# Four graph layers on one core: bias additions by accumulating DMA, an earlier place for the load of x, one more strip buffer and a new order of the steps

## Chip, cores and metric

The kernel runs on 1 core of one Trainium2 chip. The metric is the device time of one execution in microseconds, the median of three runs. A span is the time from the first to the last instruction of one profiled execution.

## The reference, cut to what matters

There are B = 32 graphs of N = 512 nodes with D = 256 features. Each passes through four layers in turn, and each layer ends in a residual and a layer norm. All is float32.

```python
x = layernorm(x + L0(x, adj))   # h = (1+eps)*x + adj @ x;  relu(h @ W1 + b1) @ W2 + b2
x = layernorm(x + L1(x, adj))   # graph attention, 4 heads, mask adj > 0.5, softmax, ... + bias
x = layernorm(x + L2(x, adj))   # attention, 8 heads of 32, scores + log(adj + 1e-6), ... @ Wo.T + bo
x = layernorm(x + L3(x, adj))   # softmax over (x W x^T) * adj with a node mask, times x
```

Three of the layers add a bias row of D numbers to every node's row: b2, bias and bo. These three additions are what the first part of the change is about.

## The kernel before

**Tiles.** A graph's x is one SBUF tile of 128 partitions by 4 chunks by 256 features, 4 KB in a partition. It is updated in place through all four layers, from its load (L667) to its store (L1436). The adjacency comes as four strips of 128 x 512, once for layer one (L660) and again for layer four (L1317). Layer one transposes the strips on TensorE (L685) into AT. Its first matmul that reads x is hT (L718), followed by h1T (L741) and y (L760).

**Tiling of TensorE.** Most matmuls use the whole 128 x 128 array. The scores of layer two's attention (s, L1105) are tiled by rows, four of 32 at once. Its sums (o_ps, L1163), and the denominators at L983, L1210 and L1232, are tiled by 32 columns, and layer one's attention (o_ps, L946) by 64 columns.

**Buffers.** There are four pools of interchangeable SBUF buffers: B (8 KB in a partition, 11 of them), C (4 KB, 12 of them: x, hT, xT, v, q, k and others take turns), D (2 KB, 17 of them: adjacency strips, nm, xs_row, exponentials of layer four) and the eight PSUM banks. A step that starts a tile takes a buffer and waits until an earlier owner is done with it.

**Order.** About six graphs are in work at once. Every piece of work is a named step with an engine, a duration, and the steps it comes after. `Plan.order` runs through them with these durations and picks, for the engine that is free, the step with the earliest due time. Due times are shifted by a table of moves that is written out in the last call, `plan.run`. The result is one fixed instruction order on each engine. So any change of a duration, of a buffer count or of the table changes the order everywhere. SyncE's DMA queue is in order too: a load that waits for its buffer holds up every load behind it.

**Bias.** `bias_bc` holds the three rows copied to all 128 partitions (3 KB in a partition). `bias_steps(k, after)` adds row k to x with four GpSimd operations, one for each chunk. Step `xb1` comes after hT, which needs x without the bias; `xb2` and `xb3` come after the transposes of x in layers two and three. The residual additions (L642, L1027) come after them.

**Denominators of layer two.** Eight tiles of exponentials are added up by accumulating DMAs that GpSimd issues (L1138, L1191), from SBUF to SBUF.

**Loads of a graph.** Steps `la0i` to `la3i` issue the four strips, and `lxi` issues x after `la3i`. `transfer` adds two steps that only count time: the queue and the landing.

Of the kernel before, what the change touches and what calls it, by code (L numbers as in the profile page):

```python
# [10 lines left out]
F32 = mybir.dt.float32  # L11
# [3 lines left out]
ALU = mybir.AluOpType  # L15
AX = mybir.AxisListType

P = 128
# [12 lines left out]
def row_bcast(ap, n):  # L31

    return bass.AP(tensor=ap.tensor, offset=ap.offset, ap=[[0, P], [1, n]])
# [194 lines left out]
def fast_path(  # L228
# [23 lines left out]
    nc = tc.nc  # L252
    B, N, D = x.shape
    NC = N // P
# [8 lines left out]
    const = ctx.enter_context(tc.tile_pool(name="const", bufs=1))  # L263
    sb = ctx.enter_context(tc.tile_pool(name="sb", bufs=1))
    small = ctx.enter_context(tc.tile_pool(name="small", bufs=1))
    dram = ctx.enter_context(tc.tile_pool(name="dram", bufs=3, space=bass.MemoryType.DRAM))
# [27 lines left out]

    wT = {n: const.tile([P, DC, D], F32, name=f"w{n}T") for n in ("q", "k", "v", "o")}
    w3_sb = const.tile([P, DC, D], F32, name="w3_sb")
    bias_bc = const.tile([P, 3, D], F32, name="bias_bc")


    def blk(i):  # L300
# [1 line left out]


    plan = Plan({
        "B": 11, "C": 12, "D": 17, "p": 8,

        "live": 6, "L0": 1, "L1": 2, "L2": 2, "L3": 1, "AT": 4, "zs": 7, "edge": 1, "tmp": 2,
    })
    step = plan.step
# [8 lines left out]
    def transfer(name, us, after, queue="q1", land=4.0):  # L318

        @step(f"{name}.q", queue, us, after)
        def _():
            pass

        @step(name, None, land, (f"{name}.q",))
        def _():
            pass


    def prepare():
        plan.graph()
        slot = plan.slot[0]
        t = {}
# [7 lines left out]
        def load(name, us, *transfers, take=(), little=False):  # L342


            @step(f"ld_{name}", "act" if little else "sp", 0.5 * len(transfers), take=take)
            def _():
                for transfer in transfers:
                    (nc.scalar if little else nc.sync).dma_start(*transfer())

            transfer(name, us, (f"ld_{name}",), "q3" if little else "q1", 2.0)  # L350
# [37 lines left out]
        load("w1", 2.5, lambda: (w1_sb, rows(w1)))  # L388
        load("w2", 2.5, lambda: (w2_sb, rows(w2)))

        def bias_row(k, b):
            return lambda: (bias_bc[:, k, :], row_bcast(b, D))

        load("bias", 0.6, *(bias_row(k, b) for k, b in enumerate((b2, gbias, bo))), little=True)

        def vector(name, a):
            def transfer():
# [159 lines left out]
    def graph(g):  # L557
# [3 lines left out]
        t = {"g": g}  # L561
# [16 lines left out]
        def bias_steps(k, after):  # L578


            @step(f"xb{k}", "pool", 2.7, after + ("^bias",))
            def _():

                for c in range(NC):
                    nc.gpsimd.tensor_tensor(  # L585
                        t["x"][:, c, :], t["x"][:, c, :], bias_bc[:, k - 1, :], ALU.add
                    )

        def norm_stats(n, c):
            nc.vector.bn_stats(t[f"st{n}"][:, c, :], t["xo" if n == 4 else "x"][:, c, :])  # L590
# [70 lines left out]

            transfer(f"la{c}", 1.0 if g == 0 else 2.0, (f"la{c}i",), land=4.0 if g else 2.0)

        @step("lxi", "sp", 0.45, (f"la{NC-1}i",), take=("C=x/2",))
        def _():
            t["x"] = mid("x", [P, NC, D], "x")
            nc.sync.dma_start(t["x"], x[g].rearrange("(c p) d -> p c d", p=P))  # L667
# [298 lines left out]
        for h in range(H1):  # L966
            after = (f"o1{h//2}0", f"zm{h}1")
            for k, m in enumerate((2, 1)):
# [6 lines left out]
                after = (f"as{h}0",)  # L975
# [470 lines left out]
    for g in range(B):  # L1446
        graph(g)
    with tc.manual_schedule():
        plan.run([(24, 0.1, 6, 100.0, ((959604, 5.0), (114893, 5.0), (536715, 2.0), (293975, 2.0), (179355, 2.0), (633130, 2.0), (136849, 2.0), (39540, 2.0)), (0.7, 0.3, 0.3), (('R', 7.0), ('Re', -17.0), ('Rl.q', 5.0), ('Rs.q', -24.0), ('Rsi', -4.5), ('Rt', -0.5), ('ab', 3.0), ('as00', -7.0), ('as01', 14.0), ('as10', 5.5), ('as11', 19.5), ('as20', -59.5), ('as21', 4.5), ('as30', -1.0), ('as31', -8.0), ('at0', 3.0), ('at1', 1.0), ('at2', 5.0), ('at3', 7.5), ('atd0', 5.0), ('atd1', -8.0), ('atd2', 0.5), ('atd3', 2.0), ('ate0', 6.0), ('ate1', 4.0), ('ate3', -93.0), ('cd1', 23.5), ('cd2', 24.0), ('cd3', 17.0), ('cd6', 34.5), ('cd7', 44.5), ('cq1', 31.5), ('cq2', 13.5), ('cq3', 2.0), ('cq5', 24.0), ('cq6', -16.0), ('cq7', -12.5), ('d1', -18.0), ('d2', -2.0), ('de', -81.5), ('dev1.0', -32.0), ('dev2.0', -18.0), ('dev3.0', -10.0), ('dev4.0', -53.0), ('e00', -9.0), ('e01', 0.5), ('e02', -5.0), ('e03', -9.5), ('e10', -17.5), ('e11', -4.5), ('e12', 3.5), ('e13', -20.0), ('e20', -111.5), ('e21', -50.0), ('e22', -3.5), ('e23', 7.5), ('e30', -17.0), ('e31', -1.0), ('e32', -16.0), ('e33', -46.0), ('e40', -115.0), ('e41', -5.0), ('e42', 7.0), ('e43', -11.0), ('e50', -8.5), ('e51', -8.5), ('e52', 3.0), ('e53', -3.0), ('e60', -13.5), ('e61', -27.0), ('e62', -6.0), ('e63', 1.0), ('e70', 7.0), ('e71', 54.5), ('e72', -2.0), ('e73', -20.0), ('ed0', 8.0), ('ed1', 11.5), ('ed2', -27.5), ('ed3', -0.5), ('f0', 10.0), ('f1', -2.0), ('f2', 3.5), ('f3', 7.0), ('fd0', 25.0), ('fd1', 6.5), ('fe0', -21.5), ('fe1', -44.5), ('fe2', -21.0), ('fe3', -12.0), ('fq0', -4.5), ('fq1', -2.0), ('h0', 0.5), ('h1', -34.5), ('he1', 4.5), ('hsb.q', -22.0), ('hsbi', 34.5), ('hsl', 10.0), ('i0', 8.5), ('i1', 6.0), ('ie0', -28.5), ('ie1', -15.5), ('k0', -31.0), ('k1', -56.5), ('ke0', 81.5), ('ke1', 87.0), ('la0.q', -176.5), ('la0i', -14.5), ('la1.q', -36.5), ('la2.q', -22.0), ('la3.q', -21.0), ('la3i', -9.0), ('lb0.q', 6.0), ('lb0i', -13.0), ('lb1.q', 4.5), ('lb1i', 38.0), ('lb2.q', 6.0), ('lb2i', -18.0), ('lb3.q', -6.0), ('lb3i', -3.5), ('ldni', -2.0), ('lx.q', 5.5), ('lxi', 8.0), ('m00', -14.0), ('m01', -4.0), ('m10', -24.0), ('m11', 2.0), ('m20', -51.5), ('m21', -8.0), ('m30', -29.0), ('m31', -19.0), ('m40', 9.0), ('m41', 4.0), ('m50', 30.0), ('m51', -2.5), ('m60', 12.5), ('m61', 28.0), ('m70', -1.0), ('m71', 2.5), ('n0', -1.5), ('n1', 2.0), ('n2', 1.5), ('n3', 4.5), ('n5', 0.5), ('n6', -28.5), ('n7', 8.5), ('nd0', 4.0), ('nd1', 36.5), ('no0', 9.0), ('no1', 8.5), ('node', 7.0), ('o100', 3.0), ('o101', -6.0), ('o110', 6.0), ('o111', 4.5), ('oe0', -1.0), ('oe1', 33.0), ('out0.q', 1.0), ('out0i', -5.5), ('p0', -2.0), ('p1', 7.5), ('q1', 1.0), ('qe0', -10.0), ('qe1', -12.0), ('r10', 119.5), ('r11', 3.5), ('r12', -10.0), ('r13', -19.0), ('r20', 161.0), ('r21', -13.0), ('r22', -3.5), ('r23', 25.0), ('r30', 83.0), ('r32', -1.0), ('r33', -6.0), ('r40', -2.0), ('r41', -12.0), ('r42', -9.0), ('rc00', 8.5), ('rc01', 3.0), ('rc10', 7.5), ('rc11', -27.0), ('rd1', -54.5), ('rd30', -59.0), ('rd31', 1.5), ('rd32', 2.5), ('s0', -1.0), ('s1', -16.0), ('s2', -0.5), ('s3', -21.5), ('s4', -35.5), ('s6', -24.5), ('s7', -2.0), ('sh1.0', -3.0), ('sh2.0', -12.5), ('sh3.0', 10.0), ('sh4.0', 7.0), ('st10', 16.5), ('st11', -1.0), ('st13', -29.5), ('st20', 15.0), ('st21', 35.5), ('st22', -0.5), ('st23', 27.5), ('st30', 50.0), ('st31', -14.0), ('st32', -9.0), ('st33', 15.5), ('st40', -4.5), ('st41', -9.5), ('st42', -2.0), ('st43', -3.0), ('t0', 0.5), ('t1', -2.5), ('t3', -12.0), ('ta0', -41.0), ('ta1', -0.5), ('ta2', -23.5), ('ta3', 3.0), ('tb0', -5.5), ('tb1', 1.0), ('tb2', 10.0), ('tb3', 23.5), ('te0', -13.0), ('te2', -5.0), ('te3', 26.0), ('u0', -1.0), ('u1', 7.0), ('u2', -2.0), ('u3', -55.0), ('ue0', -39.5), ('ue1', 16.5), ('ue2', -1.5), ('ue3', -17.0), ('v10', -3.5), ('v11', -16.5), ('v12', 5.5), ('v13', -5.0), ('v20', -50.0), ('v21', 10.5), ('v22', -10.0), ('v23', -5.0), ('va1.0', 15.5), ('va2.0', 7.5), ('va3.0', 0.5), ('va4.0', -24.5), ('ve10', -76.5), ('ve11', -11.5), ('ve12', -16.0), ('ve13', 0.5), ('ve20', -1.0), ('ve22', -23.0), ('ve23', -21.5), ('w0', 0.5), ('w1', 0.5), ('w3', 8.5), ('wx0', 32.5), ('wx1', -33.5), ('wx2', 18.5), ('wx3', 7.0), ('x10', -10.0), ('x11', 4.0), ('x30', -8.0), ('x31', -22.0), ('xb1', 1.0), ('xb2', -1.0), ('xb3', -3.5), ('xe10', -84.5), ('xe11', -134.0), ('xe20', -7.0), ('xe21', -5.5), ('xe30', -52.0), ('xe31', 12.0), ('xs.q', 10.5), ('xsi', 3.0), ('xt10', -6.5), ('xt11', -50.0), ('xt20', -73.5), ('xt21', -11.0), ('xt30', -4.0), ('xt31', 0.5), ('y0', 8.0), ('y1', -32.0), ('yd00', -41.5), ('yd01', 18.0), ('yd10', 11.0), ('yd11', 13.5), ('yn0', -82.0), ('yn1', -24.0), ('yn2', -25.0), ('yn3', -68.0), ('yt2', -0.5), ('z01', -48.5), ('z03', -6.0), ('z11', -0.5), ('z12', 2.0), ('z20', 1.0), ('z21', 2.5), ('z22', 3.0), ('z30', -57.5), ('z31', -38.0), ('z32', 5.0), ('z33', -3.0), ('zm00', -10.0), ('zm01', 29.0), ('zm11', 33.5), ('zm20', 24.0), ('zm21', 15.5), ('zm30', 10.0), ('zm31', 17.5)))])

# [470 lines left out]
```

## Time and profile before

| what | value |
|---|---|
| median of three runs | 2952.09 us (2947.92 to 2953.53) |
| the profiled execution's own time | 2948.64 us |
| its span | 2946.9 us |
| TensorE busy | 2890.2 us, 98% |
| VectorE busy | 2344.2 us, 80% |
| ScalarE busy | 1906.5 us, 65% |
| GpSimd busy | 704.4 us, 24% |
| granted TensorE clock | 0.998 |
| share of the DMA engines in the queue that GpSimd issues to | 40.7% |

In the profile, PE is TensorE's matmuls, PEld its weight loads, DVE VectorE, ACT ScalarE, POOL GpSimd, and SPq the DMA queue that SyncE issues to. `hT_ps<-AT,x L718` means that the instruction of line 718 writes hT_ps and reads AT and x. A list of waits names for each group of instructions what ended its engine's idle time, with the total, the number of waits and the longest. Where several things were waited for, the one that came last in the records is named. The chain of waits goes back from the last instruction, at each step to what released it. A wait on an engine that is not the bound costs nothing by itself.

### The profile page before, as it was taken

To read this page: it belongs to the slowest core of one execution; us is meant where nothing else is said; L and a number is where in the kernel's file an instruction comes from. 1 tells how busy PE (TensorE), PEld (TensorE's weight loads), DVE (VectorE), ACT (ScalarE), POOL (GpSimd) and SP (SyncE) were. 2 spreads that over 40 slices of the span, in tenths; PEclk is the share of its full clock that TensorE was granted. 3 is DMA by queue.
4 is the path that set the end of the run, shared out by engine and by line. 5 is a ranking of instruction groups with operands and counts; after the bars stand their busy time and mean duration, and the time that the engine had idled before them with its cause. 6 is when DMAs were issued, how large, how long until landed. Compare 5 with 4: busy or idle time off the path is not lost.

```text
span 2946.9 us, 42883 instructions
## 1 busy us (share of the span) xinstructions
PE 2890.2 (98%) x15521; PEld 1651.0 (56%) x15521; DVE 2344.2 (80%) x4389; ACT 1906.5 (65%) x3818; POOL 704.4 (24%) x782
## 2 busy tenths in 40 slices
PE   8999999999999999999999999999999999999998
PEld 6544665555655556555556555565555555555554
DVE  2878878877788877788777887778887778888796
ACT  3766766666666666666666666666576666666665
POOL 2322222122221222222222212222222222122210
PEclk9999999999999999999999999999999999999999
DMA  4166676455675456764557654567545576446651
GB/s 147 58 129 135 144 163 147 105 123 127 151 163 109 116 127 138 163 135 109 123 124 163 158 104 119 128 144 163 127 110 124 129 163 139 109 110 147 143 113 41
DMA packets 121467, 380.77 MB, mean 129 GB/s; under 512 B 12129, under 2 KB 52257, under 8 KB 89377
## 3 DMA queue, kind: packets, MB, share of 16 engines
q0 software_dynamic: 31744, 227.56, 40.7%
q1 hardware_dynamic: 88112, 149.75, 15.3%
q8 instruction: 125, 2.05, 0.3%
q10 hardware_dynamic: 1392, 0.66, 0.1%
q14 instruction: 94, 0.76, 0.1%
HBM read 133.30 MB, written 17.07 MB: 51 GB/s over the span
## 4 chain that ended last, share of the span: by engine, by line
PE 76%; DVE 14%; DMA 7%; ACT 2%; issue 1%; POOL 0%; POOLq 0%; SPq 0%; ACTq 0%; DVEq 0%
PE s L1347 8%; PE hT_ps L718 7%; PE o_ps L946 7%; PE h1T_ps L741 7%; PE y_ps L760 7%; PE s L1105 6%; DMA x<-in_x_dram 5%; PE o_ps L1163 5%; DVE z L1127 4%; PE iT_ps L1333 4%; PE v_ps L1086 3%; PE qT_ps L1068 3%; PE kT_ps L1068 3%; PE o2p_ps L1289 2%; PE xT_t L1049 2%; PE AT_t L685 2%
## 5 line engine op out<-in xcount | busy, mean ns | idle before, releaser
L1118 ACT ACTIVATE z<-s 128x512 f32<-128x512 f32 x1024 | 560.1, 605 | 164.2 <-PE o_ps L1163 107.2
L1127 DVE SCALAR_TENSOR_TENSOR z<-AT,z 128x1024 f32<-128x1024 f32 x512 | 618.1, 1216 | 48.3 <-ACT z L1118 48.2
L912 ACT ACTIVATE z<-R_bc,nT,S 128x512 f32<-128x512 f32 x512 | 390.3, 817 | 164.7 <-PE y_ps L760 138.1
L1138 POOL DMA_DIRECT2D z<-z x186 | 166.6, 898 | 1147.2 <-PE s L1105 329.1
L923 DVE SCALAR_TENSOR_TENSOR z<-z,T,edge 128x512 f32<-128x512 f32 x512 | 401.6, 829 | 45.4 <-ACT z L912 45.2
L585 POOL TENSOR_TENSOR x<-x,bias_bc 128x256 f32<-128x256 f32 x384 | 343.9, 994 | 211.4 <-PE xT_t L788 156.3
L631 ACT ACTIVATE x<-x,shift,rstd 128x256 f32<-128x256 f32 x508 | 285.1, 607 | 136.5 <-DVE shift L621 136.0
L613 POOL TENSOR_TENSOR rstd<-ve,nhalf 128x4 f32<-128x4 f32 (+1 forms) x131 | 147.7, 1128 | 806.7 <-DVE ve L607 792.9
L1105 PE MATMUL s<-qT,kT 32*128 32x512 f32 x2048 | 293.2, 639 | 4.1 <-ACT qT L1074 4.1
L1163 PE MATMUL o_ps<-z,v 128*32 128x512 f32 x2048 | 257.8, 600 | 0.2 <-DVE z L1127 0.2
L946 PE MATMUL o_ps<-z,v 128*64 128x512 f32 x1024 | 244.4, 605 | 0.2 <-DVE z L923 0.2
L1401 PE MATMUL o_ps<-x,eT 128*128 128x256 f32 x1024 | 233.5, 380 | 0.1
L1347 PE MATMUL s<-xT,iT 128*128 128x512 f32 x512 | 233.5, 599 | 0.0
L973 DVE TENSOR_TENSOR z<-z 128x1024 f32<-128x1024 f32 (+1 forms) x256 | 230.7, 953 | 2.0 <-PE o_ps L946 1.9
L741 PE MATMUL h1T_ps<-hT,w_sb 128*128 128x512 f32 x512 | 231.4, 593 | 0.0
L760 PE MATMUL y_ps<-w_sb,h1T 128*128 128x256 f32 x1024 | 226.9, 379 | 1.3 <-ACT h1T L747 1.3
L1253 DVE RECIPROCAL rdT<-rdT 128x256 f32<-128x256 f32 x128 | 221.5, 1738 | 7.1 <-ACT rdT L1246 7.1
L590 DVE BATCH_NORM_STATS2 st<-x 128x6 f32<-128x256 f32 x508 | 211.2, 416 | 9.3
L760 PEld LDWEIGHTS y_ps<-w_sb,h1T 128*128 128x128 f32 x1024 | 194.1, 190 | 39.3 <-issue 12.2
L718 PE MATMUL hT_ps<-AT,x 128*128 128x384 f32 (+2 forms) x768 | 209.8, 382 | 0.1
L1401 PEld LDWEIGHTS o_ps<-x,eT 128*128 128x128 f32 x1024 | 189.5, 190 | 30.2 <-issue 2.0
L1377 ACT ACTIVATE z<-z,nmax 128x512 f32<-128x512 f32 x128 | 92.4, 722 | 132.4 <-DVE nmax L1369 131.4
(155 smaller groups left out, 4234.8 us busy)
## 6 DMA issues: line engine op xcount, KB each, us to landing
z<-z POOLq DMA_DIRECT2D x186, 1024.0 KB, 8.1
A<-in_adj_dram SPq DMA_DIRECT2D x256, 256.0 KB
R_bc<-R_dram SPq DMA_DIRECT2D x32, 1024.0 KB
z<-z POOLq DMA_DIRECT2D x62, 512.0 KB, 6.0
x<-in_x_dram SPq DMA_DIRECT2D x32, 512.0 KB
out_dram<-x SPq DMA_DIRECT2D x31, 512.0 KB
nm<-in_nodemask_dram SPq DMA_DIRECT2D x32, 256.0 KB
xs_row<-xs_dram SPq DMA_DIRECT2D x32, 128.0 KB
```

The lines of the kernel that those rows point to most:

```text
L718: nc.tensor.matmul(ph[:, cols], t["x"][:, m, blk(d)], moving, start=(k == 0), stop=(k == len(parts) - 1),)
L741: nc.tensor.matmul(ph, w1_sb[:, d, blk(f)], t["hT"][:, d, :], start=(d == 0), stop=(d == DC - 1))
L760: nc.tensor.matmul(py[:, j, :], t["h1T"][:, f, blk(2 * c2 + j)], w2_sb[:, f, :], start=(f == 0), stop=(f == HC - 1),)
L912: nc.scalar.activation(t[f"e{h}"][:, c, :], t["Rbc"][:, h, :], AF.Relu, bias=t["nT"][:, h, c : c + 1], scale=t["S"][:, h, c : c + 1],)
L923: nc.vector.scalar_tensor_tensor(z, z, t["T"][:, h, c : c + 1], t["edge"][:, c, :], op0=ALU.add, op1=ALU.mult)
L946: nc.tensor.matmul(po[j * F1 : (j + 1) * F1, :], t["v"][:, c, h * F1 : (h + 1) * F1], t[f"e{h}"][:, c, :], start=(c == 0), stop=(c == NC - 1),
L1105: nc.tensor.matmul(pk, t["k"][hs, o, blk(c)], t["q"][hs, o, :], start=True, stop=True)
L1118: nc.scalar.activation(t[f"E{k}"][:, j, :], t[f"ps{k}{j}"], AF.Exp, scale=QSCALE)
L1127: nc.vector.scalar_tensor_tensor(z, t["AT"][:, c, None, :].to_broadcast([P, 2, N]), ADJ_EPS, z, op0=ALU.add, op1=ALU.mult,)
L1163: nc.tensor.matmul(t[f"n{o}"][32 * j : 32 * j + 32, :], t["v2"][:, c, o * P + F2 * j : o * P + F2 * (j + 1)], t[f"E{k}"][:, j, :], start=( ...
L1347: nc.tensor.matmul(pt, t["iT"][:, d, blk(c)], t["xT3"][:, d, :], start=(d == 0), stop=(d == DC - 1),)
L1401: nc.tensor.matmul(py, t[f"eT{c}"][:, blk(m)], t["x"][:, m, :], start=(m == 0), stop=(m == NC - 1),)
```

## The change

1. The bias tile in SBUF is gone. A DRAM tile `biases` holds each row four times in a line, written once by three small DMAs. For each graph and bias, GpSimd issues one DMA that reads that 4 KB line for each of the 128 partitions and adds it to x in place. The step `xb{k}` is split into `xd{k}` (the issue), `xq{k}` (the queue) and `xb{k}` (the landing).
2. `lxi` comes after `la0i`, the first strip, where it came after the last.
3. The D pool has 18 buffers where it had 17.
4. The table of moves, the seeds, the weight that the planner gives to a change of tiling mode (100.0 to 165.0) and the early starts of the last graphs are new, so every engine's order is new.

```diff
-    bias_bc = const.tile([P, 3, D], F32, name="bias_bc")
+    biases = dram.tile([3, NC, D], F32, tag="biases", name="biases", bufs=1)
...
-        "B": 11, "C": 12, "D": 17, "p": 8,
+        "B": 11, "C": 12, "D": 18, "p": 8,
...
-        def bias_row(k, b):
-            return lambda: (bias_bc[:, k, :], row_bcast(b, D))
+        def bias_rows(k, b):
+            return lambda: (
+                biases[k : k + 1], bass.AP(b.tensor, b.offset, [[0, 1], [0, NC], [1, D]])
+            )
...
-            @step(f"xb{k}", "pool", 2.7, after + ("^bias",))
+            @step(f"xd{k}", "pool", 0.95, after + ("^bias",))
             def _():
-                for c in range(NC):
-                    nc.gpsimd.tensor_tensor(
-                        t["x"][:, c, :], t["x"][:, c, :], bias_bc[:, k - 1, :], ALU.add
-                    )
+                line = biases[k - 1 : k].rearrange("o c d -> o (c d)")
+                nc.gpsimd.dma_start(
+                    t["x"].rearrange("p c d -> p (c d)"), row_bcast(line, NC * D), accum_op=ALU.add
+                )
+
+            @step(f"xq{k}", "qa", 3.0, (f"xd{k}",))
+            def _():
+                pass
+
+            @step(f"xb{k}", None, 2.5, (f"xq{k}",))
+            def _():
+                pass
...
-        @step("lxi", "sp", 0.45, (f"la{NC-1}i",), take=("C=x/2",))
+        @step("lxi", "sp", 0.45, ("la0i",), take=("C=x/2",))
...
-        plan.run([(24, 0.1, 6, 100.0, (...), (0.7, 0.3, 0.3), (('R', 7.0), ...)))])
+        plan.run([(24, 0.1, 6, 165.0, (...), (2.0, 1.1, 0.1), (('R', 0.5), ...)))])
```

## The prediction

> **What bounds the kernel now.** I read the page's first two parts, then TensorE's list of waits, then SyncE's timeline and the chain over one graph, and last the groups and the DMA parts.
>
> ```profile
> span 2946.9 us, 42883 instructions
> ...
> PE 2890.2 (98%) x15521; PEld 1651.0 (56%) x15521; DVE 2344.2 (80%) x4389; ACT 1906.5 (65%) x3818; POOL 704.4 (24%) x782
> ```
>
> TensorE is the bound, in every slice. No other engine's busy time can be saved directly: only TensorE's 56.7 us of idle time (2946.9 - 2890.2), and whatever in its busy time is not arithmetic. The list of waits says where the idle time lies (columns: total us, times, longest us):
>
> ```profile
> PE hT_ps L718 <- DMA x<-in_x_dram: 17.7, 16, 2.3
> PE hT_ps L718 <- ACT x L631: 11.4, 9, 1.9
> PE AT_t L685 <- DMA A<-in_adj_dram: 8.1, 2, 4.6
> PE s L1105 <- ACT qT L1074: 4.1, 2, 3.9
> ```
>
> The first two lines are one wait. hT is the first matmul that reads x, it has 25 waits of about 1.2 us, and where ScalarE's normalization L631 is named it had long been done, so the DMA of x came last. Together 29.1 us, half of all the idle time. The other two are the ramp-up: 8.1 us is the first A, 4.1 us lies at 182 us. A further 7.9 us is the drain after the last matmul. Why x is late shows in SyncE's timeline of one graph and in the chain at the same place:
>
> ```profile
> 551.41 13.81 SPq L1317 DMA_DIRECT2D A<-in_adj_dram  x4
> 581.08 0.38 SPq L667 DMA_DIRECT2D x<-in_x_dram  x1
> ```
>
> ```profile
> 581.04 0.04 ACT v L815
> 581.08 9.26 DMA x<-in_x_dram
> 590.34 0.14 issue
> 590.48 7.22 PE hT_ps L718 x40
> ```
>
> The load is not held up by the four pieces of A ahead of it (issued some 70 us earlier). It is held until ScalarE's copy of v (L815) frees a C buffer, is issued 0.04 us after that, needs 9.26 us, and hT starts 0.14 us after it lands. In the built order TensorE has 8.8 us of its own work between that buffer's release and hT: 9.4 - 8.8 leaves the 0.7 us wait of this graph; where the load takes 10 to 11 us the wait is 1.5 to 2.
>
> **What the Trainium skill says.** "TensorEngine Tiling (Array Packing)", section Key Properties: changing the tiling mode, not merely the tile, drains TensorE. The trace agrees: a 512-column all-array matmul starts the next one after 0.429 us, but 0.523 us where a tiled one follows, 0.094 us more. "SBUF — State Buffer", section SBUF: two separate sides: VectorE and GpSimd share a port pair that is locked for a whole instruction. It agrees too: of the 512 operations at L923, 115 overlap a bias addition on GpSimd for at least 30% of their time and take 1.11 us in the mean, the 372 without overlap 0.75. "DMA: Bandwidth & Descriptors", section Anatomy of one DMA, fits 2.0 us plus bytes/436e3 to a DMA issued by GpSimd: 3.2 us for 512 KB as an estimate. The trace has 6.0 for its accumulating DMA of that size, so I use the trace.
>
> **The change part by part.**
>
> ```profile
> L585 POOL TENSOR_TENSOR x<-x,bias_bc 128x256 f32<-128x256 f32 x384 | 343.9, 994 | 211.4 <-PE xT_t L788 156.3 <-DMA w_sb<-in_L_gnn_W_dram 17.1 <-PE hT_ps L718 17.0
> ...
> q0 software_dynamic: 31744, 227.56, 40.7%
> ...
> z<-z POOLq DMA_DIRECT2D x186, 1024.0 KB, 8.1
> ...
> z<-z POOLq DMA_DIRECT2D x62, 512.0 KB, 6.0
> ```
>
> (1) *Bias additions.* 384 GpSimd additions go (343.9 us of GpSimd); 96 accumulating DMAs come, each 0.87 us to issue (row L1191: 866 ns), 84 us. GpSimd falls from 704 to about 445 us. TensorE never waits for it, so this is worth 0 directly. VectorE gets back about 42 us at L923 (115 x 0.37) and more elsewhere, but at 80% it is not the bound: 0. The cover is TensorE's own work; if it went, VectorE at about 2250 us would be next, far behind. The new latency: 6.0 to 8.1 us by the two rows above, plus 0.9 of issue. The nearest reader is the residual x after y_ps (xb1): in the new order 23.5 us of TensorE work lie between the last hT and the point where VectorE may use it, so 7 to 9 us are hidden. xb2 and xb3 have over 50 us. An accumulating DMA from DRAM is not in this trace: as little as 3.2 us, and up to 23 us, cost nothing; beyond that x normalizes late. On GpSimd's queue each one stands before a rstd power or a z accumulation and delays it by 0.9 us, less than the 4 x 1.0 us before.
>
> (2) *DMA load.* q0 used 40.7% of 16 x 2946.9 us over 27,776 data packets (186 x 128 + 62 x 64), so 0.69 us for one of 8 KB. The new ones carry 4 KB: 0.35 us as an estimate, 24 per engine and graph, 8.3 us per 88.5 us. The share in mid-run goes from 0.59 (window 450 to 540) to 0.68. No saturation: 0.
>
> (3) *x behind the first piece of A.* In mid-run the edit does nothing by itself: in the new order too x stands behind all four pieces. What moves it is the new order: its C buffer is now freed by the last s matmul of L1347, leaving 19.6 us of TensorE work until hT instead of 8.8. Loads of 9.3 to 10.9 us fit. Gain: 29.1 less the 0.5 of the first graph, 28.6. Behind x on SyncE now stand nm, the four A pieces of layer four, R_dram and R_bc. The A pieces have 88 us until VectorE reads them, nm 15; R_bc comes 11.8 us after x's issue and shares x's landing semaphore, so it waits for x to land, which 10.9 still meets; R_bc has 15.0 us of TensorE work until ScalarE uses it, against 12.4 before. No cost.
>
> (4) *The new order on TensorE.* I count the runs of equal tiling mode in both built orders, and read from single start times what a run costs beyond its matmuls: row-tiled (L1105) 1.071 us for one group and 1.930 for two, so 0.212; 32-column (L1163) 0.137; 64-column (L946) 0.152; all-array 0.094. Runs go 253 to 225, 207 to 224, 91 to 94 and 230 to 182: -5.9 + 2.3 + 0.5 - 4.5 = -7.7 us. The matmuls are the same.
>
> (5) *18 strips*: one more D buffer, in the place of the bias tile (3 KB of a partition). The A loads already come 42 us before use: 0.
>
> (6) *Start.* The first x now stands behind 512 KB of w1 on SyncE: at about 360 GB/s in the busy slices to 14 us, +1.5; 384 KB of bias rows shrink to 12 KB: -1.1. Net +0.4, between -1 and +2.
>
> Other waits are unknown, since all engines are reordered. In mid-run the smallest distance in TensorE work between a VectorE or ScalarE step's release and the matmul needing it is 1.4 us in the new order and 0.9 in the old, and 14 such pairs of steps are under 3 us against 27: no tighter. I take 0, with -9 (ramp waits go) to +15.
>
> Sum: -28.6 - 7.7 + 0.4 = -35.9 against the profiled execution's own 2948.64 us (span plus 1.7), 2912.7. The median shown is 3.45 us above that execution, so 2916.
>
> **The rivals.**
> A, the forecast (0.68): 2916, own range 2902 to 2930.
> B, a wait in the place of x's (0.15): once hT isn't late, h1T, y and the normalization come sooner, while the ScalarE exponentials and VectorE's products set when s and o_ps can start. For it: VectorE at 80% and pairs 1.4 us apart. Against it: the old order had closer pairs and no such wait in mid-run. Half of 28.6 comes back: 2930, at worst 2942.
> C, no net change (0.05): the new order gains nothing in mid-run, because C buffers are the scarce thing and x holding one 11 us longer makes another step wait for it as long: 2952 - 7.7 + 7 of new ramp waits, about 2951.
> D, slower (0.12): the DRAM-to-SBUF accumulation saturates the DMA engines. The skill's DMA page, section SWDGE vs HWDGE vs iDMA, has both kinds of queue served in turn by the same engines, so x, A and R_bc would all slip. For it: every one of 128 rows reads the same 4 KB of DRAM, not seen here as an accumulation. Against it: R_bc, also one row read by 128, lands well. It decides from (89.1 - 52.2)/24 = 1.54 us a packet, 4.5 times my estimate; each further 0.1 us adds 2.4 us to each of 28 graphs, 67 us. At 1.65 us: 2990.
>
> **How the numbers follow.** About 0.2%, 5.9 us, is what a measurement of this kernel can tell from no change. A and B are faster: 0.83. C is the same for 0.04 and slower for 0.01; with D, 0.13. The range 2902 to 2942 holds nearly all of A and B and leaves out C and D.
>
> **What would show it.** Right: hT's wait for x gone from TensorE's list, x issued about 19 us before hT, mid-run hT starts about 89.0 us apart (now mean 90.4), TensorE's busy time near 2882 us, GpSimd near 445, q0 near 49%, x<-biases landing in 6 to 8 us. Wrong: a new row of several microseconds per graph in TensorE's list (B, C), or x<-biases landing after more than 20 us and R_bc waits on ScalarE (D).

## The result, and the profile after

The changed kernel takes 2910.59 us in the median (2910.01 to 2911.59, four runs), the kernel before beside it 2951.36 us (four runs): a ratio of 0.9863 with an interval of 0.9846 to 0.9880, 40.8 us less. The forecast was 2916 (2902 to 2942). The profiled execution took 2910.6 us, 38.0 less than that of the kernel before, which lay 2.7 us under its median.

The page of the kernel after, its parts on engines, queues and DMA issues:

```profile
span 2908.8 us, 42662 instructions
...
PE 2878.8 (99%) x15521; PEld 1655.2 (57%) x15521; DVE 2256.4 (78%) x4389; ACT 1903.9 (65%) x3818; POOL 454.9 (16%) x494
...
q0 software_dynamic: 45568, 277.89, 49.2%
...
x<-biases POOLq DMA_DIRECT2D x96, 512.0 KB, 7.1
```

TensorE's busy time fell by 11.4 us and its idle time from 56.7 to 30.0. Its list of waits after (total us, times, longest us):

```profile
PE AT_t L695 <- DMA A<-in_adj_dram: 4.9, 1, 4.9
PE hT_ps L728 <- DMA x<-in_x_dram: 4.5, 1, 4.5
PE o_ps L956 <- DVE y L1028: 2.1, 1, 2.1
```

Of hT's 25 waits for x one is left, that of the first graph. SyncE's timeline over one graph shows why (start us, us):

```profile
1062.15 2.47 SPq L670 DMA_DIRECT2D A<-in_adj_dram  x4
1108.27 0.38 SPq L677 DMA_DIRECT2D x<-in_x_dram  x1
```

hT starts at 1127.43, 19.2 us after x is issued; in the graph that the prediction showed it was 9.4. Over the 24 mid-run graphs (hT from 411 to 2490 us before, from 417 to 2460 us after) the starts lie 88.81 us apart in the mean, 90.42 before. Over these 23 distances that is 37.1 us of the 38.1 by which the span fell; ramp and drain together gave 1.0.

x is also faster once it is issued. The trace keeps every DMA packet, and x's are the 512 packets of 1 KB in SyncE's queue behind its issue. In the mean of those 24 graphs the first one starts 3.1 us and the last one ends 5.3 us after the issue (7.7 at most). In the kernel before these are 4.6 and 9.2 us.

### The profile page after: what moved, and what is told of

The parts are those of the page before. It is cut to its first block, busy times and chain, and to the rows that moved or that the text cites. A ratio compares the mean times of both kernels' runs of the same rounds, so it can differ in the third digit from the quotient of the medians.

```text
span 2908.8 us, 42662 instructions
## 1 busy us (share of the span) xinstructions
PE 2878.8 (99%) x15521; PEld 1655.2 (57%) x15521; DVE 2256.4 (78%) x4389; ACT 1903.9 (65%) x3818; POOL 454.9 (16%) x494
## 3 DMA queue, kind: packets, MB, share of 16 engines
q0 software_dynamic: 45568, 277.89, 49.2%
## 4 chain that ended last, share of the span: by engine, by line
PE 95%; DMA 2%; ACT 1%; DVE 1%; issue 0%; POOL 0%; POOLq 0%; ACTq 0%; SPq 0%
PE s L1115 9%; PE o_ps L1173 8%; PE hT_ps L728 8%; PE o_ps L1411 8%; PE s L1357 8%; PE y_ps L770 8%; PE o_ps L956 7%; PE h1T_ps L751 7%; PE iT_ps L1343 4%; PE v_ps L819 4%; PE o2p_ps L1299 4%; PE kT_ps L1078 4%; PE qT_ps L1078 4%; PE v_ps L1096 4%; PE xT_t L1059 2%; PE eT_t L1396 2%
## 5 line engine op out<-in xcount | busy, mean ns | idle before, releaser
L1137 DVE SCALAR_TENSOR_TENSOR z<-AT,z 128x1024 f32<-128x1024 f32 x512 | 603.0, 1207 | 36.4 <-ACT z L1128 36.0
L933 DVE SCALAR_TENSOR_TENSOR z<-z,T,edge 128x512 f32<-128x512 f32 x512 | 363.7, 747 | 157.7 <-ACT z L922 156.9
L641 ACT ACTIVATE x<-x,shift,rstd 128x256 f32<-128x256 f32 x508 | 296.1, 609 | 152.0 <-DVE shift L631 152.0
L1173 PE MATMUL o_ps<-z,v 128*32 128x512 f32 x2048 | 267.4, 602 | 1.8 <-DVE z L1137 1.7
L1357 PE MATMUL s<-xT,iT 128*128 128x512 f32 x512 | 226.6, 594 | 0.7 <-ACT z L1128 0.7
L770 PEld LDWEIGHTS y_ps<-w_sb,h1T 128*128 128x128 f32 x1024 | 194.1, 190 | 27.9 <-issue 0.8
L1115 PEld LDWEIGHTS s<-qT,kT 32*128 32x128 f32 x2048 | 86.0, 183 | 166.0 <-ACT z L1128 118.8
L825 ACT COPY v<-v_ps 128x264 f32<-128x264 f32 x128 | 47.9, 376 | 183.7 <-PE v_ps L819 183.2
```

Source lines behind the costliest of these rows:

```text
L770: nc.tensor.matmul(py[:, j, :], t["h1T"][:, f, blk(2 * c2 + j)], w2_sb[:, f, :], start=(f == 0), stop=(f == HC - 1),)
L933: nc.vector.scalar_tensor_tensor(z, z, t["T"][:, h, c : c + 1], t["edge"][:, c, :], op0=ALU.add, op1=ALU.mult)
L1115: nc.tensor.matmul(pk, t["k"][hs, o, blk(c)], t["q"][hs, o, :], start=True, stop=True)
L1137: nc.vector.scalar_tensor_tensor(z, t["AT"][:, c, None, :].to_broadcast([P, 2, N]), ADJ_EPS, z, op0=ALU.add, op1=ALU.mult,)
L1173: nc.tensor.matmul(t[f"n{o}"][32 * j : 32 * j + 32, :], t["v2"][:, c, o * P + F2 * j : o * P + F2 * (j + 1)], t[f"E{k}"][:, j, :], start=( ...
L1357: nc.tensor.matmul(pt, t["iT"][:, d, blk(c)], t["xT3"][:, d, :], start=(d == 0), stop=(d == DC - 1),)
```

## The experiments

All ratios are to the kernel before on the same chip, where it took 2949.2 to 2951.4 us. "Distance" is the mean distance of the hT starts of those 24 graphs in the profiled execution. Times from x's issue are counted from the start of the issue; the expectations of e6 and e9 count TensorE's work from its end, which gives 8.3 us where the text below has 8.7.

| kernel | median us | ratio (interval) | distance us |
|---|---|---|---|
| before | 2951.36 | 1 | 90.42 |
| after | 2910.59 | 0.9863 (0.9846 to 0.9880) | 88.81 |
| e1, old order, x in 4 KB rows | 2942.26 | 0.9969 (0.9958 to 0.9979) | 90.18 |
| e2, old order, biases by DMA | 2932.72 | 0.9933 (0.9917 to 0.9950) | 89.74 |
| e3, new order, biases on GpSimd | 2971.38 | 1.0082 (1.0052 to 1.0112) | 90.87 |
| e4, new order, x late | 3108.69 | 1.0535 (1.0518 to 1.0553) | 95.97 |
| e5, old order, no biases | 2930.36 | 0.9929 (0.9913 to 0.9946) | 89.87 |
| e6, old order, one sum cut | 2905.88 | 0.9847 (0.9831 to 0.9864) | 88.97 |
| e7, new order, more modes | 2950.42 | 1.0001 (0.9992 to 1.0010) | 90.43 |
| e8, new order, 17 strips | 2911.66 | 0.9868 (0.9852 to 0.9885) | 88.81 |
| e9, e2 with two sums behind x | 2992.15 | 1.0160 (1.0128 to 1.0192) | 92.06 |
| e10, first x ahead of w1 | 2908.84 | 0.9864 (0.9847 to 0.9880) | 88.81 |
| e11, biases in 1 KB packets | 2926.85 | 0.9921 (0.9902 to 0.9939) | 89.16 |

**e1: is it x's load that the old kernel waits for?** The old order, but each partition takes one row of 4 KB in place of four of 1 KB.

```diff
-            nc.sync.dma_start(t["x"], x[g].rearrange("(c p) d -> p c d", p=P))
+            nc.sync.dma_start(t["x"], x[g].rearrange("(p c) d -> p c d", p=P))
```

> The kernel before with its order untouched; only the load of x is laid out as 128 rows of 4 KB in place of 512 rows of 1 KB (nodes are numbered otherwise than in adj, so the output is not the reference's). If the late landing of x is what the change took away, a load of 5 to 7 us in place of 9.3 fits into the 8.8 us of TensorE work after the buffer's release, hT's wait goes and the time falls by 26 to 33 us to about 2921. If the order as a whole, or GpSimd's additions, were the cause, it stays within 3 us of 2951.

Measured: 2942.26, 8.6 us less and not 30. The mean time from x's issue to hT went from 9.87 to 9.56 us only, and the end of x's last packet (of 128 of 4 KB here) from 9.2 to 8.9. So a quarter of the row count hardly shortens the load: it isn't mainly its own rows that take 9 us.

**e2: what does the accumulating DMA do alone?** The old order and 17 strips, with the bias part of the change only.

```diff
-                for c in range(NC):
-                    nc.gpsimd.tensor_tensor(
-                        t["x"][:, c, :], t["x"][:, c, :], bias_bc[:, k - 1, :], ALU.add
-                    )
+                line = biases[k - 1 : k].rearrange("o c d -> o (c d)")
+                nc.gpsimd.dma_start(
+                    t["x"].rearrange("p c d -> p (c d)"), row_bcast(line, NC * D), accum_op=ALU.add
+                )
```

> The kernel before with its order and its 17 strips; only the bias additions are made by the accumulating DMA. If the additions lie beside TensorE's work, as predicted, it stays at 2951 within 4 us, GpSimd falls to about 445 us and VectorE by 60 to 100 us. The rival, that GpSimd's additions slow VectorE through the shared port and VectorE's lateness is what TensorE pays for, gives 2930 or less.

Measured: 2932.72, 18 us less. Valued at 0, this part alone brings nearly half of what the whole change gains. TensorE's waits in e2:

```profile
PE hT_ps L719 <- DMA x<-in_x_dram: 15.2, 14, 4.2
PE AT_t L686 <- DMA A<-in_adj_dram: 4.9, 1, 4.9
PE s L1106 <- ACT qT L1075: 3.3, 1, 3.3
```

The old 29.1 us of hT's waits are 15.2, 4.2 of them in the first graph. In the 24 mid-run graphs the idle time ahead of hT, with the pauses too short for the list, is 12.2 us, against 28.7. In both kernels TensorE has 8.7 us of work between x's issue and hT; what changed is how soon after its issue x lets hT start, 9.2 us in the mean where it was 9.9. VectorE's busy time fell by 89 us, but that is no direct gain: in mid-run TensorE of the kernel before waits nowhere but at hT.

**e3: the same question in the new order.** The changed kernel with the four additions by c on GpSimd again; order and everything else as after.

> The changed kernel in its own order, with the bias additions back on GpSimd, four to a step. By the prediction 0 to 3 us slower than the changed kernel: 2911 to 2914, with VectorE about 90 us busier. By the rival of the shared port 2930 or more.

Measured: 2971.38 (2962.44 to 2990.85), 61 us above the changed kernel and above the kernel before. In TensorE's list of waits there is a new first row, the copy of hT by ScalarE:

```profile
PE h1T_ps L748 <- ACT hT L732: 25.8, 11, 5.2
```

The timeline of one such place, VectorE, ScalarE and GpSimd only (start us, us, and in brackets the engine's idle time ahead of it and what ended that):

```profile
609.76 0.92 POOL L1145 DMA_DIRECT2D z<-z  x1 [6.58 <-DMA z<-z]
610.39 1.35 POOL L620 TENSOR_TENSOR rstd<-ve,nhalf 128x4 f32<-128x4 f32 x1
611.41 5.74 POOL L584 TENSOR_TENSOR x<-x,bias_bc 128x256 f32<-128x256 f32 x8
611.77 5.41 DVE L628 SCALAR_TENSOR_TENSOR shift<-mv,rstd 128x4 f32<-128x4 f32 x1 [4.76 <-POOL rstd L620]
...
617.22 1.09 ACT L638 ACTIVATE x<-x,shift,rstd 128x256 f32<-128x256 f32 x2 [11.06 <-DVE shift L628]
```

GpSimd's queue stands for a z sum to land, the power of the normalization (rstd) comes late behind it, and eight additions follow at once. While they run, VectorE's `shift`, 0.16 us elsewhere, takes 5.41 us, ScalarE idles 11.06 us, and TensorE finds no hT. Thus the new order, as it was built, needs the accumulating DMA. The profiled execution is 55 us longer than that of the changed kernel: 29.5 us more idle time of TensorE and 25.8 us more busy time, with the granted clock at 0.50 in five stretches of mid-run, 27 us in all. The loss isn't divided up between the late queue and the held VectorE.

**e4: what does a late x cost?** The changed kernel, x issued behind R's store of the graph before.

```diff
+            x, r = at[g, "lxi"], at[g - 1, "Rsi"]
+            if x < r < at[g, "h0"]:
+                order.insert(r, order.pop(x))
```

> The changed kernel in which x is issued only after R of the graph before it is stored, 7.8 us of TensorE work before hT in place of 19.6; nothing else is moved. If x's place is the main term, each of some 26 graphs waits 1.5 to 2.5 us: 2950 to 2970. If other parts of the new order bring the gain, it stays at 2911 within 5 us.

Measured: 3108.69, 198 us above the changed kernel; far more than expected. In mid-run TensorE has only 5.6 us of work between x's issue and hT where 7.8 were expected, x's last packet ends 10.1 us after the issue, and TensorE idles 5.1 us ahead of hT in each graph. Then it runs slowly. Windows around one such hT, which starts at 1384.4 (window, its length, busy time of each engine, granted TensorE clock, DMA share, GB/s):

```profile
1372.00:1384.00 12.00, 6.88 (x40) 5.89 (x38) 9.73 (x35) 4.84 (x10) 1.50 (x2) 0.99 1.00 221
1384.00:1386.00 2.00, 1.56 (x4) 1.27 (x5) 0.16 (x1) 0.00 (x0) 1.52 (x2) 0.50 1.13 389
1386.00:1388.00 2.00, 2.00 (x10) 1.67 (x9) 0.00 (x0) 0.00 (x0) 0.00 (x0) 0.68 1.01 213
1388.00:1390.00 2.00, 2.00 (x13) 1.55 (x12) 0.00 (x0) 0.41 (x1) 0.00 (x0) 1.00 1.02 213
```

The granted clock is 0.50 and then 0.68 in the first two windows of 2 us after the pause, and in the 24 graphs hT's matmuls take 8.4 to 10.0 us instead of 6.99. So 5.1 us of idle time cost 7.16 us a graph (95.97 - 88.81), an estimated 186 us in 26 graphs. That the new order needs x early is shown. But the edit moves two things at once: x gets less time, and it comes to a place where the DMA engines are full (share 1.00 to 1.13) and takes 10.1 us where the changed kernel has 5.3. The two weren't separated.

**e5: is it the DMA that helps in e2, or the absence of the additions?** The old kernel with nothing in the additions' place.

```diff
-                for c in range(NC):
-                    nc.gpsimd.tensor_tensor(
-                        t["x"][:, c, :], t["x"][:, c, :], bias_bc[:, k - 1, :], ALU.add
-                    )
+                pass
```

> The kernel before with its 384 bias additions on GpSimd left out and nothing in their place; the three bias rows are not added to x. It tells what gave the 18 us that the accumulating DMA alone brought in the old order. Theory 1, the additions are in the way (GpSimd's queue is blocked by them and VectorE is held while they run, so that the z accumulation issued 3.5 us ahead of x comes 0.6 us later than it could): the gain stays without any DMA, about 2932, between 2925 and 2935; VectorE's busy time falls to about 2255 us as it did with the DMA. Theory 2, the gain came with the DMA itself (its traffic or its places in the queue change when the others land): without it the time is back at 2951 (2947 to 2955). Nothing of the 18 us was predicted: the prediction valued the bias part at 0.

Measured: 2930.36, as fast as e2. So it is the additions on GpSimd that cost, and the DMA that replaces them is nearly free. The traces point to the way. The z accumulations that GpSimd issues ahead of x come earlier: in most mid-run graphs of the kernel before 9.5, 3.5 and some 2 us ahead of x, in e5 11.1, 4.2 and some 3.5 (the first stood behind four additions on GpSimd's queue, the second waits for a VectorE product). hT starts 0.6 us sooner after x is issued. That the earlier sums are the cause isn't tested by itself, and which counts for more, the queue or VectorE, wasn't separated.

**e6: does x wait in the DMA engines behind those accumulations?** The old kernel, additions on GpSimd as ever; the 1 MB sum issued 3.5 us ahead of x is cut to 16 columns.

```diff
                 src, dst = (t[f"E{b}"].rearrange("p h n -> p (h n)") for b in (k, a))
+                if k == 5:
+                    src, dst = src[:, :16], dst[:, :16]
                 nc.gpsimd.dma_start(dst, src, accum_op=ALU.add)
```

> The kernel before, with the z accumulation that GpSimd issues 3.5 us ahead of x (the fifth head group's, 1 MB) cut to its first 16 columns in every graph, so that its issue, its wait and its semaphore stay and its 1 MB of traffic goes; the rest of that sum is left out. The DMA share is about 1.0 while x lands. Theory 1, x stands in the DMA engines behind that accumulation: x lands in some 7 us instead of 9.3, the 8.3 us of TensorE work ahead of hT cover it, hT's wait goes, and the time falls by the 29 to 33 us of it, to 2919 (2915 to 2925). Theory 2, the 9.3 us are x's own 512 rows, or R_bc that is issued 5.5 us behind it: x still lands in 9 us or more and the time stays at 2951 (2945 to 2954).

Measured: 2905.88, a larger gain than expected (9 of the 43 us of span lie in ramp and drain) and 4.7 us under the changed kernel, with a sum left out. In TensorE's list, of the waits for x only the first graph's is left:

```profile
PE AT_t L685 <- DMA A<-in_adj_dram: 6.9, 2, 4.6
...
PE hT_ps L718 <- DMA x<-in_x_dram: 0.7, 1, 0.7
```

x's first packet now starts 2.3 us after the issue in the mean and its last ends after 4.9, where these were 4.6 and 9.2. Until x's first packet, GpSimd's queue alone takes 0.96 of the DMA engines in the kernel before. So theory 1 holds: x was late because of the accumulation ahead of it. The windows of one graph of the kernel before, in which x is issued at 671.0 and lands at 681.2, have the DMA share in their last column but one:

```profile
671.00:673.00 2.00, 2.00 (x20) 0.73 (x22) 1.90 (x9) 1.91 (x8) 0.00 (x0) 1.00 1.01 197
673.00:675.00 2.00, 2.00 (x18) 0.84 (x10) 2.00 (x6) 1.52 (x4) 0.00 (x0) 1.00 0.95 139
675.00:677.00 2.00, 2.00 (x11) 1.77 (x10) 1.97 (x4) 0.00 (x0) 0.34 (x1) 1.00 1.30 184
677.00:679.00 2.00, 2.00 (x11) 1.77 (x10) 0.99 (x5) 0.00 (x0) 1.34 (x2) 1.00 0.64 150
679.00:681.00 2.00, 0.68 (x4) 0.25 (x2) 1.68 (x6) 1.52 (x4) 0.25 (x1) 1.00 1.18 289
```

The share is 1.0 in the mean of these five (a packet counts with its whole time in the window in which it starts, so one window can pass 1), while the mean over a whole graph, which the prediction used, was 0.59. e6 also measures the old order without the wait: 88.97 us a graph. Hence the wait was worth (90.42 - 88.97) x 23 = 33.4 us, and what the new order saves beyond it in mid-run is (88.97 - 88.81) x 23 = 3.7 us.

**e7: the price of a change of mode.** The changed kernel with three sums of layer two taken apart in TensorE's order.

```diff
+                for moved, place in ((n4, yt), (n5, u0)):
+                    order.remove(moved)
+                    order.insert(order.index(place), moved)
+                order.remove(w0)
+                order.insert(order.index(u1) + 1, w0)
```

> The changed kernel with three sums of layer two taken apart on TensorE in 24 graphs: the same matmuls, but four more changes of tiling mode in a graph. The price used in the prediction (0.212 us for a run of row-tiled matmuls, 0.137 for a 32-column one, 0.152 for a 64-column one, 0.094 for an all-array one) gives 0.462 us a graph, 11 us in all: 2922 (2918 to 2926), all of it in TensorE's busy time and none in its list of waits. If a change of mode costs nothing that isn't hidden by the weight loads: 2911 (2909 to 2913). If moving the sums makes another engine late: over 2930, with a new row in TensorE's list of waits.

Measured: 2950.42, 39.8 us more and not 11: the third case, two new waits in each of the 24 graphs.

```profile
PE o_ps L1189 <- ACT v L841: 13.4, 24, 0.6
PE eT_t L1412 <- ACT z L1403: 9.4, 24, 0.4
```

TensorE's busy time rose by 16.1 us, 0.67 a graph. If each of the two waits also ends an overlap of 0.16 us between neighbouring matmuls, as the one at hT did, 0.35 us are left; the predicted 0.46 lies between, but the run doesn't measure it alone. What it shows surely is how thin the new order's margins are: a few sums moved among their neighbours cost as much as the whole change brings.

**e8: the 18th strip.** The changed kernel with `"D": 17`; the order of all instructions is the same, only which buffer they get.

> The changed kernel with 17 strips instead of 18; the order of all instructions is the same, only which buffer each strip gets. The prediction valued the 18th strip at 0: 2911 (2909 to 2913). If the earlier release matters in the new order, an A load comes late or VectorE and ScalarE wait for a strip, and the time rises by over 3 us, with the mid-run hT starts over 88.9 us apart.

Measured: 2911.66 (2910.23 to 2913.23), against 2910.59 (2910.01 to 2911.59); the profiled spans are 2908.6 and 2908.8. No difference.

**e9: could the old order be kept, with the sums behind x?** e2, with a small GpSimd instruction that reads v put ahead of the two z sums, and both issued behind x in 24 graphs.

```diff
+            moved = [order[c], order[f]]
+            order[x + 1 : x + 1] = moved
+            del order[f], order[c]
...
+    def gate(g):
+        some = vs[g][:, NC - 1, :4]
+        nc.gpsimd.tensor_tensor(gated, some, some, ALU.add)
```

> The old order with the accumulating DMAs of the biases (the kernel that took 2932.7), and in 24 graphs the two z accumulations that GpSimd issued 4.1 and 1.7 us ahead of x are held until v, whose last copy falls with x's issue, is written: they stand behind x in the DMA engines instead of ahead. Nothing is left out. Theory 1, x is late because of what stands ahead of it in the engines and not because its C buffer comes late: it lands within the 8.3 us, hT's wait goes, mid-run hT starts are 89.0 us apart instead of 89.7, and the time is 2915 (2908 to 2919). Theory 2, only less traffic helps, since all queues are served in turn: x lands as late as before, 2930 to 2935. Theory 3, the two sums, 5 to 6 us later, make the strips or the later sums late: over 2936, with a new row in TensorE's list of waits.

Measured: 2992.15, slower than the kernel before. hT waits for x in the first graph only, and x's last packet ends 3.7 us after the issue. Here no traffic is left out, so the place of the sums is enough to make x late or not, and theory 1 is right about x. But in each of the 24 graphs TensorE waits 2.2 us at another place, and the distance is 92.06 us:

```profile
PE v_ps L1108 <- ACT xT L1075: 53.2, 24, 3.8
PE AT_t L706 <- DMA A<-in_adj_dram: 4.7, 1, 4.7
PE hT_ps L739 <- DMA x<-in_x_dram: 4.5, 1, 4.5
```

The chain of waits at one of them (start us, us):

```profile
595.07 6.82 DMA R_dram<-R_rows
...
602.03 11.49 DMA R_bc<-R_dram
...
614.32 2.21 ACT z L934 x3
616.53 1.15 ACT h1T L768 x2
617.68 0.48 ACT xT L1075
...
618.20 1.71 PE v_ps L1108 x4
```

The sums that no longer delay x delay R_bc. It is issued 1.6 us later behind x than in e2, and its last packet ends 11.3 us after its issue in the mean, where that was 7.5. ScalarE's exponentials wait for it, and the copy of xT that TensorE needs is queued behind them on ScalarE. The expectation had named the strips and the later sums for such a loss; it is R_bc. So moving both sums right behind x doesn't serve x and R_bc in time in the old order; moving only one of them wasn't tried. The new order instead gives x twice the time.

**e10: the first graph's x.** The changed kernel with that one load ahead of w1.

```diff
+        at = {s[:2]: i for i, s in enumerate(order)}
+        order.insert(at[0, "ld_w1"], order.pop(at[1, "lxi"]))
```

> The changed kernel with the first graph's x issued ahead of w1 on SyncE instead of behind it; all else is the same. The prediction charged 1.5 us for that place of x: 2909.5 (2908.5 to 2910.5), with the one wait of hT for x down from 4.5 us to about 3. If w1 is needed as early as x, the wait moves to h1T and nothing is gained: 2910.6 (2910 to 2912).

Measured: 2908.84 (2908.18 to 2910.59). The trace has what was meant: hT's start waits fall from 4.5 to some 2 us, the first mid-run hT starts at 414.44 instead of 416.94, and from there on both run 88.81 us a graph. The two weren't timed side by side, and their ratios to the kernel before (0.9864 and 0.9863) are the same, so the times don't show that this version is the better one.

**e11: how much room have the DMA engines?** The changed kernel with four times the packets for the same bias bytes.

```diff
-                line = biases[k - 1 : k].rearrange("o c d -> o (c d)")
+                row = biases[k - 1 : k, 0, :]
...
-                    t["x"].rearrange("p c d -> p (c d)"), row_bcast(line, NC * D), accum_op=ALU.add
+                    t["x"], bass.AP(row.tensor, row.offset, [[0, P], [0, NC], [1, D]]), accum_op=ALU.add
```

> The changed kernel with the accumulating DMAs of the biases in packets of 1 KB instead of 4 KB (each of 128 partitions reads the row of 1 KB four times): the same bytes, four times the packets, 96 more packets per engine and graph. It doses the rival in which the DMA engines saturate. By the prediction's slack (23.5 us of TensorE work until the sum is read, and the DMA engines at 0.67 in mid-run): it lands some microseconds later than 7.1, nothing waits, 2911 (2910 to 2914). If the DMA engines have no room for it: R_bc, A or the sums of z come late, and the time is over 2930, with ScalarE or VectorE waiting for a DMA in mid-run.

Measured: 2926.85, 16 us more; between the two cases. q0's share went only from 49.2 to 53.9%, but the additions land after 11.4 us instead of 7.1, the 1 MB sums after 10.9 instead of 8.5, and TensorE waits at kT, in six mid-run graphs and three times in ramp and drain, once for 4.4 us:

```profile
PE kT_ps L1078 <- ACT xT L1063: 11.4, 9, 4.4
```

The chain at one of the six:

```profile
1129.60 14.15 DMA R_dram<-R_rows
...
1143.83 6.15 DMA R_bc<-R_dram
...
1152.99 0.96 ACT xT L1063 x2
...
1153.99 1.98 PE kT_ps L1078 x4
```

A store of 8 KB takes 14.15 us to land, R_bc follows it, and again ScalarE comes late. In the changed kernel R_bc leaves 8.2 us behind this store in the mean and 10.0 at most. Each issue also keeps GpSimd for 1.41 us instead of 0.91, but the chain doesn't run through GpSimd. About half of the loss lies in mid-run (0.35 us a graph); the first mid-run hT alone comes 8 us later. Rival D's mechanism exists, and it begins to cost far below the saturation from which the prediction let it decide.

## Why the prediction was right, and where it wasn't

The forecast's sum was 35.9 us, and 38.0 us came between the two profiled executions (40.8 between the medians). The case was A, as forecast, and the main cause was the forecast one. That the sum came so near is in part luck, since the errors of its terms offset each other:

- **The wait for x (step 3), forecast 28.6 us, measured 33.4.** The mechanism was right: x's C buffer, the 19.2 us, the wait gone, hT 88.81 us apart where 89.0 was forecast. The size was low since the list counts idle time alone. In a graph that waits, hT also loses its overlap of 0.16 us with the matmul before, and its burst, up to the start of the matmul behind it, takes 7.06 us instead of 6.99: 0.23 us in each graph, 5.3 us in 23, which with the 27.9 us of idle time ahead of these 23 starts makes 33.2. The step took the load's 9.3 to 10.9 us as its own length; at its new place x needs 5.3, so most of the 19.2 us is margin. R_bc was said to be issued 11.8 us behind x; it goes out 20.6 us behind it, and nothing waits for it on TensorE. TensorE's work ahead of hT before was 8.7 us in the trace, not 8.8.
- **The mode changes (step 4), forecast 7.7, measured 3.7 in mid-run** and at most 1.0 more with everything else at the ends. Between e6 and after, both without mid-run waits for x, TensorE's busy time differs by 4.3 us; the other 7.1 of its 11.4 us less went with the wait, since e6 has them too. The step counted mode runs over the whole program and took them all as time. In a mid-run graph the traces have one row-tiled and one all-array run less and one 32-column run more (7, 5 and 7 where there were 8, 6 and 6), which at the step's own prices is 0.17 us, 3.9 us in 23. So the prices fit what mid-run shows, though no run measures them alone; the other half of the 7.7 lies in ramp and drain, and didn't show as time there.
- **The bias additions (step 1), forecast 0: this is the step that failed.** "At 80% it is not the bound: 0" looked at engine shares. The additions cost 18 us in the old order (e2, e5) and 61 us in the new order (e3). In the old order x lands later with them, judging by the traces because they delay the z sums that stand ahead of x in the DMA engines. In the new order they stand in the normalization's way. GpSimd and VectorE don't bound this kernel, but they set when transfers start. The 18 us are not to be added to the 33.4: by the distances of e2, (90.42 - 89.74) x 23, 15.6 us of them are part of the same wait.
- **DMA load (step 2), forecast 0.** The total came out right (49.2% on q0, landing 7.1 us where 6 to 8 was forecast; GpSimd's busy time fell to 454.9 us where 445 was), and TensorE waits for none of these DMAs in mid-run in the kernel after. "No saturation" was read from the mean of a graph; where x lands the engines were full before the change already (share 1.0 in the mean of the five windows), and that, not x's own rows (e1), made the 9.3 us. e11 shows that the margin left is small.
- **x behind the first piece of A (step 3), forecast no effect in mid-run.** It holds: with the new table, the kernel built with the old line is instruction for instruction the same program, so the edit isn't the cause of anything. "An earlier place for the load of x" comes from the new order alone.
- **18 strips (step 5), forecast 0:** 0 (e8). **Start (step 6), forecast +0.4:** hT of the first graph starts at 13.04 instead of 12.85, +0.2; x's place behind w1 costs 2.5 us in the trace (e10), more than the 1.5; what gave most of that back at the first hT, perhaps the smaller bias load, wasn't tried. The time after TensorE's last matmul rose from 7.85 to 9.96 us, which no step had. Larger shifts hide in the 1.0 us of the ends: the first mid-run hT starts 6.3 us later (416.94 against 410.63), and the stretch behind the last mid-run hT start is 7.3 us shorter. Neither was forecast or explained.
- **Rivals.** B, a new mid-run wait: none in the changed kernel, but it is what e7 and e9 turn into when a few steps are moved. C: no. D: not in the changed kernel; in e11 some of it, x<-biases landing after 11.4 us and not over 20.

## What to carry to other kernels

When a load is late, look at the DMA share in the microseconds in which it lands and at what was issued ahead of it, not at the mean of the stage: an engine that is never the bound can still put its transfers in the way. Moving transfers only helps if what then shares the engines with them has room; x served first made R_bc late. And take a wait's worth from start-to-start distances: the list of waits leaves out lost overlap and, after long pauses, a slower clock.

## What the runs showed of the hardware

- In e4's 24 mid-run graphs, after a pause of TensorE of 4.7 to 6.0 us, the granted clock is 0.50 until some 3 to 6 us after hT's start, and the 40 matmuls of hT take 8.4 to 10.0 us instead of 6.99. After mid-run pauses of up to 1.9 us they take 7.06 in every graph; of the few pauses of 2.1 to 2.3 us, two were followed by 8.7 us, with the clock at 0.50 for 3.4 us (e1, e5), and two by 7.06 (before, e5). The Trainium skill, "TensorE: Matmul & The Clock Gate", Part 1, describes such a gate: half the clock after an idle window, released by some microseconds of work. The windows of e4 agree.
- A VectorE instruction of 0.16 us took 5.41 us beside eight GpSimd additions of 128x256 that followed one another (e3). Without the additions VectorE's busy time is 88 us less for the same number of instructions in the same order (2344.2 in the kernel before, 2256.1 in e5).
- An 8 KB store took 13.2 to 14.2 us to land in the six mid-run graphs of e11 that wait at kT, where the biases travel in 1 KB packets. In the changed kernel, with 4 KB packets, R_bc leaves 8.2 us behind this store in the mean.
- With one accumulation of 1 MB in SBUF issued 3.5 us ahead of it, a 512 KB load had its last packet at 9.2 us after the issue in the mean; without that traffic it was 4.9 us (e6). In e9 two accumulations are issued 1.0 and 1.6 us behind the load instead of 4.2 and some 2 us ahead of it (e2), and the last packet ends after 3.7 us instead of 8.6.
